# Layer 3 of a four-layer graph network: even bursts of four head units and one outer unit, one accumulator each, and tasks placed by array shape

## The chip, the cores and the metric

The kernel runs on one core of one Trainium2 chip. A core has a matrix engine (PE, with its weight loads shown apart as PEld), a vector engine (DVE), an activation engine (ACT), GpSimd (POOL), and DMA queues, here fed by SyncE (SP). Each engine works through its own instructions in program order and waits for others by semaphores. The metric is the device time of the program in microseconds. Three runs of the kernel before gave 2006.18 to 2008.17 us, median 2007.85.

## The reference

The program is four graph layers over x (16 batches, 1024 nodes, 64 features), with one adjacency matrix; after each layer comes x = layernorm(x + layer(x)). The change touches the fourth, called layer 3:

```
mask = graph + eye(N) > 0
h = einsum('bnc,hdc->bhnd', x, Wh)                 # four heads of 64
out_h = gat(h, mask, bh)                           # per head: softmax over masked h h^T, times h
cat = concatenation of the four heads              # 256
z = leaky_relu(cat, 0.2)
h2 = einsum('bnk,dk->bnd', z, Wo)                  # 64
out2 = gat(h2, mask, bo)                           # the outer attention
z2 = leaky_relu(out2, 0.2)
out = (z2 - mean) * rsqrt(var + 1e-5) * gamma + beta
x = layernorm(x + out)
```

`gat(h)` takes scores h h^T, drops the masked ones, takes a softmax over the neighbours and multiplies by h. Batch b's outer attention needs all four of its heads.

## The kernel before

Names: B = 16 batches, E = 15 the last; P = 128 partitions; N = 1024 nodes, HALF = 512; C = 8 chunks of 128 nodes; D = 64. The four heads are NP = 2 pairs n = 0, 1, the two heads of a pair in the two halves of the 128 partitions.

**Units.** A head unit (`heads`, L1327) is one chunk k of neighbours and one half h of the nodes, for both heads of a pair: two score products into a PSUM tile `s` (L1336; 64 rows by 128 columns of the array each, side by side), an exponential on ACT into `e` (L1340), a multiplication by the adjacency on DVE (`mask`, L1344), and two products with the values into an accumulator y (L1351; 128 rows by 64 columns each). A pair has 16 units: eight chunks for h = 0, then eight for h = 1. Batch b has 32. An outer unit (`head_out`, L1471) is one chunk of the outer attention, with the same four steps and one more on DVE, which adds up the rows (`add_up`, L1489), as the outer attention has no spare column for its sums. Batch b has eight. In the trace each product of 32-bit numbers is two records, so a unit has four records of scores and four of products.

**PSUM.** Pool `ps_s` has three tiles of two banks, tag "s". Scores and every other product of the tasks below take them in turn. Pool `ps_h` has two accumulators, acc0 and acc1. L1349 chooses: pair 0 uses acc0 for h = 0 and acc1 for h = 1, pair 1 uses acc0 for both, and the outer attention acc1. When an accumulator is complete, ACT copies it out (yT, L1358; y2T, L1523).

**Bursts.** The plan (from L1937) cuts the units into bursts, eight for a batch: four of five head units, then four of three head units; in the latter, from batch 1 on, two outer units of the batch before are put between the head units. After batch 15 two bursts with its outer units follow (five and three, LAST = 5). `run` (L1951) emits a burst as: `catch_up` (small steps left over), the scores and exponentials of its units, the tasks of `mids`, the products of the burst before (`drain`), the masks of its own units, and the tasks of `slots`. PE, ACT, DVE and POOL keep this order (`manual_schedule`); the adjacency and sum checks at the end of the program are outside of it.

**Tasks.** Per pair: `project_T` (poT, L1378, shape 64 by 64) turns yT into zT, `inverse` takes the reciprocal of the sums through DRAM, `quotient` multiplies and applies the leaky ReLU. Per batch: `h_2T` (ph2T, L1452, 128 by 64) makes h2 and swaps its halves on DVE; `shift_of` (pn, L1273, 128 by 128) finds the largest norm, whose negative goes into the exponential (DVE, then POOL, then ACT); `h_2v` (ph2v, L1465, 64 by 128) transposes h2 for the values. Then the ends: `gather` (po, L1534, 128 by 128), `layer`, `mean`, `centre`, `scale`, `affine`, `residual`, `mean`, `centre`, `scale`, `finish`, nearly all on DVE, with two small ACT instructions (ln_rstd) after `scale`, which it appends to `roots`; and a Newton step on DVE at the next `catch_up`. Per two batches: `prep_x` (pxT, 128 by 128), `prep_h` (phT, L1310, 64 by 128), `prep_sq`, `prep_v`. Lists of places (from L1850) say in which burst and in which of `mids` and `slots` each task stands. `nodes_adj` (L1253) loads the adjacency for the outer attention in eight pieces, into tiles of the tag "e", and converts it.

The places for the last batches are lists of their own, and the tail after the last burst is an order written out by hand (`ended`, `rest`).

Of the kernel before, what the change touches and what calls it, by code (L numbers as in the profile page):

```python
# [582 lines left out]
def fast_path(  # L583
# [49 lines left out]
    def xb(b):  # L633
        return xg[b // GB][:, :, b % GB, :]
# [61 lines left out]
    def bc_mid(ap, n):  # L696

        return ap.unsqueeze(1).to_broadcast([P, n, ap.shape[1]])
# [98 lines left out]
    def drain():  # L797
        while waiting:
            waiting.pop(0)()
# [451 lines left out]


    def nodes_adj(c):  # L1253
        a_sb = l3.tile([P, N], I32, tag="e", name=f"adj3_{c}", bufs=11)
        nc.sync.dma_start(a_sb, adj_v[c])

        def convert():
            nc.vector.tensor_scalar(
                aN[:, c, :].rearrange("p (k q) -> p k q", q=P), a_sb.rearrange("p (q k) -> p k q", k=C),
                0.0, None, ALU.is_gt,  # L1260
            )
            own = aN[:, c, c * P : (c + 1) * P]
            nc.vector.tensor_tensor(own, own, ident16, ALU.max)

        return convert
    xT2, hTs, shifts, vals, zs, zTs = {}, {}, {}, {}, {}, {}

    def shift_of(key, sq):

        pn = one_bank("pn")  # L1270
        n = sq.shape[1] // P
        for c in range(n):
            nc.tensor.matmul(  # L1273
                pn[:, 2 * c : 2 * c + 2], sq[:, c * P : (c + 1) * P], pair_ones, start=True, stop=True
            )
        top = small.tile([P, 1], F32, tag="top", name="top")
        nc.vector.tensor_reduce(top, pn[:, : 2 * n], AX.X, ALU.max)  # L1277
        gtop = small.tile([P, 1], F32, tag="gtop", name="gtop")
        nc.gpsimd.partition_all_reduce(gtop, top, P, bass_isa.ReduceOp.max)  # L1279
        sh = small.tile([P, 1], F32, tag="shift", name="shift", bufs=6)  # L1280
        shifts[key] = sh

        def below():
            nc.scalar.activation(sh, gtop, AF.Identity, bias=headroom, scale=-1.0)


        soon.append(below)
# [33 lines left out]
    def prep_sq(b, n, h):  # L1321
        cols = slice(h * HALF, (h + 1) * HALF)
        for i in range(2):
            hT, sq = hTs[b + i, n]
            nc.scalar.activation(sq[:, cols], hT[:, cols], AF.Square)

    def heads(b, n):  # L1327
# [18 lines left out]

        def product(k, h, e):
            if k == 0:
                held[h] = ps_h.tile([P, HALF], F32, tag=f"acc{h * (1 - n)}", name=f"y_{b}_{n}_{h}")  # L1349
            for i in range(2):  # L1350
                nc.tensor.matmul(  # L1351
                    held[h][i * D : (i + 1) * D, :], vals[b][:, k, :], e[:, i, :],
# [46 lines left out]
        def project(q):  # L1399

            if q == 0:
                zs[b] = l3.tile([P, C, P], F32, tag="e", name=f"z_{b}", bufs=11)
            pt = ps_s.tile([P, 2, HALF], F32, tag="s", name="po")
            o = pt[:, :, : 2 * (P + 2)].rearrange("p t (c f) -> p t c f", c=2)
            for j in range(CH):
# [24 lines left out]
        return units, [project_T, inverse, quotient]  # L1430


    BURSTS, LAST = 8, 5

    def prep_out(b):

# [6 lines left out]
        def h_2T():  # L1443


            hT = l3.tile([P, 2, HALF], F32, tag="h2T", name=f"h2T_{b}", bufs=1)
            sq = l3.tile([P, HALF], BF16, tag="h2sq", name=f"h2sq_{b}", bufs=1)
            hTs[b] = hT, sq
            pt = one_bank("ph2T")
            for n in range(NP):  # L1450
                for h in range(2):
                    nc.tensor.matmul(  # L1452
                        pt[h * D : (h + 1) * D, :], woT[:, n], zTs[b][:, n, h * HALF : (h + 1) * HALF],
                        start=(n == 0), stop=(n == NP - 1),
                    )
            nc.scalar.copy(hT[:, 0, :], pt)
            nc.scalar.activation(sq, hT[:, 0, :], AF.Square)
            nc.vector.tensor_copy(hT[:D, 1, :], hT[D:, 0, :])
            nc.vector.tensor_copy(hT[D:, 1, :], hT[:D, 0, :])

# [5 lines left out]
            nc.scalar.copy(v, pt)  # L1466
            vals["out", b] = v

        return z_T, h_2T, h_2v

    def head_out(b):  # L1471
        held = {}
# [365 lines left out]

    slots, mids = {}, {}
    work = [[heads(b, n) for n in range(NP)] for b in range(B)]
    outs = [(prep_out(b), head_out(b)) for b in range(B)]
    E = B - 1

    def at(b, j, task, where=slots):
        where.setdefault((b, j), []).append(task)

    for c in range(C):
        convert = {}  # L1850
        at(0, c, lambda c=c, convert=convert: convert.update(go=nodes_adj(c)))
        at((c + 1) // BURSTS, (c + 1) % BURSTS, lambda convert=convert: convert["go"]())
    for b in range(B):
        z_T, h_2T, h_2v = outs[b][0]
        chain = [
            *work[b][0][1], *work[b][1][1], *([z_T] if b == E else []), h_2T,
            lambda b=b: shift_of(b, hTs[b][1]), h_2v,
        ]
        ends = outs[b][1][1]

        places = [(5, mids), (5, mids), (5, slots), (9, mids), (9, mids), (9, slots), (10, mids), (11, mids), (12, mids)]
        places += [(18, mids), *((j, slots) for j in (18, 19, 19, 20, 22, 24, 24, 24, 25, 28))]
        if b == E - 2:
            places[9:] = [(17, mids), *((j, slots) for j in (17, 17, 18, 18, 20, 20, 21, 22, 22, 24))]
        elif b == E - 1:
            places[9:] = [(j, slots) for j in (15, 15, 15, 15, 15, 17, 17, 17, 18, 18)]
        elif b == E:
            places[3] = 7, mids
            places[4:] = [(j, slots) for j in [7] * 5 + [10] * 11]
        for task, (j, where) in zip(chain + ends, places):  # L1870
            t = min(j // BURSTS, E - b)
            at(b + t, j - t * BURSTS, task, where)


    ended = slots[E, BURSTS - 1]
    slots[E, BURSTS - 1] = [ended[i] for i in (5, 0, 1, 6, 2, 3, 7, 8, 9, 4)]
    rest = slots[E, BURSTS + 2]
    slots[E, BURSTS + 2] = [*rest[2:4], rest[0], *rest[4:7], rest[1], *rest[7:]]
    for b in (E - 1, E):
        at(E, 2, lambda b=b: nc.vector.tensor_tensor(xb(b), xb(b), bc_mid(beta, C), ALU.add))  # L1880
    ahead = []
    for b in range(0, B, 2):
        for t, j, task, where in (
            (-1, 3, lambda b=b: prep_x(b), mids),
            (-1, 4, lambda b=b: prep_h(b, 0, 0), mids), (-1, 4, lambda b=b: prep_sq(b, 0, 0), mids),
            (-1, 5, lambda b=b: prep_h(b, 0, 1), mids), (-1, 5, lambda b=b: prep_sq(b, 0, 1), mids),
            (-1, 6, lambda b=b: prep_v(b), slots),
            (-1, 6, lambda b=b: shift_of((b, 0), hTs[b, 0][1]), mids),
            (-1, 7, lambda b=b: shift_of((b + 1, 0), hTs[b + 1, 0][1]), mids),
            (0, 0, lambda b=b: prep_h(b, 1, 0), mids), (0, 0, lambda b=b: prep_sq(b, 1, 0), mids),  # L1890
            (0, 1, lambda b=b: prep_h(b, 1, 1), mids), (0, 1, lambda b=b: prep_sq(b, 1, 1), mids),
            (0, 2, lambda b=b: shift_of((b, 1), hTs[b, 1][1]), mids),
            (0, 4, lambda b=b: shift_of((b + 1, 1), hTs[b + 1, 1][1]), mids),
            (0, 6, lambda b=b: prep_v(b + 1), slots),
        ):
            if b + t < 0:
                ahead.append(task)
            else:
                at(b + t, j, task, where)

    gat = ExitStack()
    gp = gat.enter_context(tc.tile_pool(name="gat2", bufs=2, reuse_waits="tile"))
# [11 lines left out]
        ending = l2_go(extra)  # L1914
    gat.close()
    for j, task in enumerate(ending):
        at(0, j, task)

# [9 lines left out]
    aN = l3.tile([P, C, N], BF16, tag="aN", name="aN", bufs=1)  # L1930
    dram = ctx.enter_context(tc.tile_pool(name="dram", bufs=2, space=bass.MemoryType.DRAM))

    def tasks(where, b, j):
        for task in where.get((b, j), []):
            task()

    plan = []  # L1937
    for b in range(B):
        units = work[b][0][0] + work[b][1][0]
        outer = outs[b - 1][1][0] if b else []  # L1940
        for j in range(BURSTS):
            n = 5 if j < 4 else 3
            burst, units = units[:n], units[n:]
            if j >= 4:
                for i, unit in enumerate(outer[2 * (j - 4) : 2 * (j - 3)]):
                    burst.insert(1 + 2 * i, unit)
            plan.append((b, j, burst))
    units = outs[E][1][0]
    last = [(E, BURSTS, units[:LAST]), (E, BURSTS + 1, units[LAST:])]

    def run(plan):  # L1951
        for b, j, burst in plan:
            catch_up()
            made = [(unit, unit[0]()) for unit in burst]
            tasks(mids, b, j)
            while roots:
                roots.pop(0)()
            drain()
            made = [(product, mask(e)) for (_, mask, product), e in made]
            waiting.extend(lambda product=product, e=e: product(e) for product, e in made)  # L1960
            if (b, j, burst) == plan[-1]:
                drain()
            tasks(slots, b, j)

    with tc.manual_schedule(engines=in_order):
        run(plan)
        run(last)
        for task in [catch_up, *slots[E, BURSTS + 2]]:
            task()


# [73 lines left out]
```

## Time and profile before

The profiled execution took 2005.96 us; its span, from first to last instruction of the core, is 2003.7 us, and the granted PE clock was 0.981 over it.

| stretch (us) | what it is |
|---|---|
| 0 to 650 | layers 0 to 2 |
| 650.0 to 806.95 | layer 3, bursts 0 to 16 |
| 806.95 to 1862.1 | bursts 17 to 120 |
| 1862.1 to 1928.0 | bursts 121 to 126 |
| 1928.0 to 1961.3 | burst 127, and what lies between it and the last outer attention |
| 1961.3 to 2003.7 | last outer attention, and the ends of batches 14 and 15 |

Bursts are counted from 0. A line of PE's timeline gives the start in microseconds, the time that the records take, the line, the tiles written and read with their array shape, and the number of records merged; in brackets stands how long the engine stood idle before, and what ended that. A burst's length is the distance from its first scores to those of the next burst. Some groups of layer 3: masks of heads (L1344) 512 instructions, 599.0 us; exponentials of heads (L1340) 512, 542.6 us; products (L1351) 2048 records, 494.0 us; scores (L1336) 2048 records, 497.3 us.

### The profile page before, as it was taken

The page shows a single profiled execution, that of the slowest core. Times are in us where ns is not written, and L with a number is a line of the kernel's source. Part 1 is how long each engine was busy: PE and PEld are TensorE (multiplying, and loading weights), DVE is VectorE, ACT ScalarE, POOL GpSimd, SP SyncE. Part 2 cuts the span into 40 slices and gives each one's busy share as a digit, 9 for nine tenths or more (in the row PEclk, how much of TensorE's full clock was granted, in tenths as well). Part 3 has the DMA queues.
Part 4 walks back from the last instruction along what each step waited for, and adds up shares of the span by engine and source line. Part 5 has one row for each costly group of instructions (what it writes and reads, how often), then busy time and mean ns, then how long its engine had stood idle before and what let it go on. Part 6 is the DMA issues. An engine that isn't in the chain of part 4 may idle for free.

```text
span 2003.7 us, 25793 instructions
## 1 busy us (share of the span) xinstructions
PE 1891.7 (94%) x9545; PEld 768.3 (38%) x9545; DVE 1764.4 (88%) x2930; ACT 1333.4 (67%) x2343; POOL 81.9 (4%) x77
## 2 busy tenths in 40 slices
PE   7999989998888999999999999999999999999985
PEld 3444447763332333333333333333333333333322
DVE  5899988879999868798898899989989899889996
ACT  5356567767776766676767766766677676776543
POOL 0000000000000000000000000000000000000001
PEclk8999989999999999999999999999999999999997
DMA  7000000000000210000000000000000000100000
GB/s 175 1 1 1 1 1 1 1 1 1 1 1 11 66 31 12 12 22 17 12 17 27 12 17 12 20 26 12 17 12 27 17 12 17 28 12 17 11 17 18
DMA packets 45603, 35.89 MB, mean 18 GB/s; under 512 B 37279, under 2 KB 37344, under 8 KB 45470
## 3 DMA queue, kind: packets, MB, share of 16 engines
q1 hardware_dynamic: 45166, 34.14, 6.6%
q8 instruction: 77, 1.26, 0.3%
q14 instruction: 56, 0.46, 0.1%
q10 hardware_dynamic: 304, 0.03, 0.0%
HBM read 29.45 MB, written 4.70 MB: 17 GB/s over the span
## 4 chain that ended last, share of the span: by engine, by line
PE 61%; DVE 24%; ACT 11%; issue 3%; DMA 1%; POOL 0%; SPq 0%; POOLq 0%; DVEq 0%; ACTq 0%
PE y L1351 16%; PE s L1336 14%; DVE e L1344 8%; DVE e L991 7%; PE y_l L1003 6%; PE po L1776 5%; ACT e L1340 5%; PE y L1504 4%; PE u_l L1015 3%; PE s L1479 3%; ACT e L1484 2%; PE ph2T L1452 1%; PE phT L1310 1%; PE poT L1378 1%; ACT x L780 1%
## 5 line engine op out<-in xcount | busy, mean ns | idle before, releaser
L1340 ACT ACTIVATE e<-s,shift 128x1024 f32<-128x1024 f32 x512 | 542.6, 1119 | 320.1 <-PE s L1336 320.0
L1344 DVE TENSOR_TENSOR e<-e,aT 128x1024 f32<-128x1024 f32 x512 | 599.0, 1215 | 14.8 <-ACT e L1340 14.6
L1351 PE MATMUL y<-e,vals 128*64 128x512 f32 x2048 | 494.0, 605 | 12.5 <-ACT yT L1358 5.9
L1336 PE MATMUL s<-hT 64*128 64x512 f32 x2048 | 497.3, 605 | 1.4 <-ACT e L1340 0.9
L991 DVE SCALAR_TENSOR_TENSOR e<-G_l,q,aT 128x1024 f32<-128x1024 f32 x256 | 315.3, 1275 | 3.9 <-ACT G_l L968 3.9
L1336 PEld LDWEIGHTS s<-hT 64*128 64x128 f32 x2048 | 186.3, 186 | 290.4 <-issue 153.3
L1003 PE MATMUL y_l<-e,vals_l 128*64 128x512 f32 x1024 | 254.2, 616 | 26.9 <-DVE e L991 20.1
L1351 PEld LDWEIGHTS y<-e,vals 128*64 128x64 f32 x2048 | 135.9, 137 | 303.8 <-issue 205.0
L1497 DVE TENSOR_TENSOR e<-e,aT 128x1024 f32<-128x1024 f32 x128 | 156.3, 1225 | 10.4 <-ACT e L1484 1.0
L1489 DVE SCALAR_TENSOR_TENSOR junk<-e,aN 128x1024 bf16<-128x1024 f32 x120 | 146.1, 1217 | 0.0
L1484 ACT ACTIVATE e<-s,shift 128x1024 f32<-128x1024 f32 x128 | 142.0, 1116 | 0.2 <-PE s L1479 0.2
L1504 PE MATMUL y<-e,h2v 128*64 128x512 f32 x512 | 131.6, 597 | 0.6 <-DVE e L1497 0.6
L1479 PE MATMUL s<-h2T 64*128 64x512 f32 x512 | 130.7, 591 | 0.0
L1003 PEld LDWEIGHTS y_l<-e,vals_l 128*64 128x64 f32 x1024 | 62.3, 138 | 160.4 <-issue 75.7
L1776 PE MATMUL po<-hi,aR 128*128 128x512 f32 x256 | 102.7, 402 | 11.2 <-ACT hi L1705 7.3
L1279 POOL PARTITION_ALL_REDUCE gtop<-top x48 | 55.1, 1148 | 1302.0 <-DVE top L1277 996.5
L1776 PE MATMUL po<-lo,aR 128*128 128x512 f32 x256 | 101.1, 396 | 0.0
L780 ACT ACTIVATE x<-m,bn_shift,bn_rstd 128x64 f32<-128x64 f32 x256 | 88.5, 430 | 0.0
L1479 PEld LDWEIGHTS s<-h2T 64*128 64x128 f32 x512 | 49.9, 186 | 60.0 <-issue 26.2
L1383 ACT COPY zT<-poT 64x512 f32<-64x512 f32 x124 | 71.9, 580 | 1.3 <-PE poT L1378 0.2
L1504 PEld LDWEIGHTS y<-e,h2v 128*64 128x64 f32 x512 | 36.5, 137 | 76.0 <-issue 54.0
L978 ACT ACTIVATE vals_l<-x,p 128x64 f32<-128x64 f32 (+1 forms) x256 | 64.3, 339 | 0.0
(252 smaller groups left out, 1874.9 us busy)
## 6 DMA issues: line engine op xcount, KB each, us to landing
r<-inverse SPq DMA_DIRECT2D x62, 256.0 KB
adj<-in_adj_dram SPq DMA_DIRECT2D x16, 512.0 KB
x<-in_x_dram SPq DMA_DIRECT2D x16, 256.0 KB
out_dram<-res SPq DMA_DIRECT2D x16, 256.0 KB
rows<-yT SPq DMA_DIRECT2D x62, 4.0 KB
sums<-rows SPq DMA_DIRECT2D x31, 8.0 KB
inverse<-rt SPq DMA_DIRECT2D x31, 8.0 KB
wl<-in_L_gnn_Wh_dram SPq DMA_DIRECT2D x2, 64.0 KB
```

The costliest lines, as they stand in the source:

```text
L991: nc.vector.scalar_tensor_tensor(e, G[b - b % 2][:, b % 2, :], pq[b - b % 2][1][:, k, b % 2 : b % 2 + 1], aT[:, k, :], ALU.max, ALU.mult,)
L1003: nc.tensor.matmul(held["y"][h * D : (h + 1) * D, :], vals[b][:, k, :], e[:, h * HALF : (h + 1) * HALF], start=(k == 0), stop=(k == C - 1),)
L1336: nc.tensor.matmul(s[:, i, :], hT[rows, k * P : (k + 1) * P], hT[rows, cols], start=True, stop=True)
L1340: nc.scalar.activation(e, s, AF.Exp, bias=shifts[b, n])
L1344: nc.vector.tensor_tensor(e, e, bc_mid(aT[:, k, h * HALF : (h + 1) * HALF], 2), ALU.mult)
L1351: nc.tensor.matmul(held[h][i * D : (i + 1) * D, :], vals[b][:, k, :], e[:, i, :], start=(k == 0), stop=(k == C - 1),)
L1479: nc.tensor.matmul(s[:, i, :], hT[rows, (i + k // CH) % 2, k % CH * P : (k % CH + 1) * P], hT[rows, 0, :], start=True, stop=True,)
L1484: nc.scalar.activation(e, s, AF.Exp, bias=shifts[b])
L1489: nc.vector.scalar_tensor_tensor(junk.rearrange("p c q -> p (c q)").bitcast(BF16), e.rearrange("p i q -> p (i q)"), 1.0, aN[:, k, :], ALU. ...
L1497: nc.vector.tensor_tensor(e, e, aT[:, k, :].rearrange("p (i q) -> p i q", i=2), ALU.mult)
L1504: nc.tensor.matmul(held["o"][h * D : (h + 1) * D, :], vals["out", b][:, k, :], e[:, h, :], start=(k == 0), stop=(k == C - 1),)
L1776: nc.tensor.matmul(po.rearrange("p q k f -> p (q k f)"), aR[:, k, ic * P : (ic + 1) * P], e[:, k].rearrange("p q k f -> p (q k f)"), start ...
```

## The change

The units, their arithmetic and the tasks stay; only their grouping and order in layer 3 change, and some buffers.

- Bursts: twelve of four head units; then 112 of four head units and one outer unit at the end; then five with 4+1, 3+2, 3+2, 3+2 and 3+1 units, outer units between the head units; then the last outer attention (five and three). The outer attention of batch b takes one unit in each of the bursts 8b+12 to 8b+19.
- Accumulators: acc0 for all heads, acc1 for the outer attention.
- Three places in a burst: TOP before the scores, MID between scores and products, END after the products and masks. Within a place an order number sorts the tasks. Tasks with the scores' shape (phT, ph2v) go to END, ahead of the next scores; ph2T goes to the end of MID, ahead of the products; pn, pxT and po go to the start of MID. The `roots` are emptied after MID and END instead of after `mids` alone.
- `h_2T` gives up the swap, which becomes a task of its own one place later; the h2T tile gets two buffers.
- Both shifts of a pair of batches are found in the same MID.
- The adjacency is loaded two pieces at a time, into the buffer of tag "zT", and converted one burst later; z of the last batch takes the tag "xT".
- In the last three bursts the products are not drained ahead of the masks but after them, so that the last outer attention's first five units are finished before the scores of its last three.
- `scale` of batch 13 stands at the END of bursts 127 and 129, its `affine` and first `residual` at the END of 128 and in MID of 129.

```diff
     def nodes_adj(c):
-        a_sb = l3.tile([P, N], I32, tag="e", name=f"adj3_{c}", bufs=11)
-        nc.sync.dma_start(a_sb, adj_v[c])
+        a_sb = l3.tile([P, 2, N], I32, tag="zT", name=f"adj3_{c}", bufs=1)
+        for i in range(2):
+            nc.sync.dma_start(a_sb[:, i, :], adj_v[c + i])
...
-                held[h] = ps_h.tile([P, HALF], F32, tag=f"acc{h * (1 - n)}", name=f"y_{b}_{n}_{h}")
+                held[h] = ps_h.tile([P, HALF], F32, tag="acc0", name=f"y_{b}_{n}_{h}")
...
-            hT = l3.tile([P, 2, HALF], F32, tag="h2T", name=f"h2T_{b}", bufs=1)
+            hT = l3.tile([P, 2, HALF], F32, tag="h2T", name=f"h2T_{b}", bufs=2)
...
+        def swap():
+            hT = hTs[b][0]
             nc.vector.tensor_copy(hT[:D, 1, :], hT[D:, 0, :])
             nc.vector.tensor_copy(hT[D:, 1, :], hT[:D, 0, :])
...
+    TOP, MID, END = range(3)
+
+    def at(burst, place, task, order=5):
+        table.setdefault((burst, place), []).append((order, len(table.get((burst, place), [])), task))
...
+        places = [(5, MID, 3), (5, MID, 4), (7, MID, 4)]
+        if b < E:
+            chain = [*chain, *work[b][1][1], h_2T, swap, lambda b=b: shift_of(b, hTs[b][1]), h_2v]
+            places += [(9, MID, 3), (9, MID, 4), (9, END, 5), (10, MID, 8), (10, END, 5), (11, MID, 0), (12, END, 8)]
+        if b < E - 1:
+            chain = [*chain, *ends]
+            if b < E - 2:
+                places += [
+                    (21, MID, 1), (21, END, 5), (22, MID, 5), (22, END, 5), (23, MID, 5), (24, MID, 5), (24, END, 5),
+                    (25, MID, 5), (26, END, 5), (27, MID, 5), (28, END, 5),
+                ]
+            else:
+                places += [
+                    (21, MID, 1), (21, END, 5), (22, END, 5), (23, MID, 5), (23, END, 5), (24, END, 8), (25, MID, 5),
+                    (25, END, 5), (25, END, 5), (25, END, 5), (26, END, 8),
+                ]
+        for task, (j, place, order) in zip(chain, places):
+            at(g + j, place, task, order)
...
+            (-5, END, 9, lambda b=b: prep_h(b, 0, 0)), (-4, MID, 6, lambda b=b: prep_sq(b, 0, 0)),
+            (-4, END, 9, lambda b=b: prep_h(b, 0, 1)), (-3, MID, 6, lambda b=b: prep_sq(b, 0, 1)),
+            (-3, END, 6, lambda b=b: prep_v(b)),
+            (-2, MID, 0, lambda b=b: shift_of((b, 0), hTs[b, 0][1])),
+            (-2, MID, 0, lambda b=b: shift_of((b + 1, 0), hTs[b + 1, 0][1])),
...
-                n = 5 if j < 4 else 3
...
+    kinds = ["hhhh"] * 12 + ["hhhho"] * (Q * (E - 1) - 4)
+    kinds += ["hhhho"] * 4 + ["hhhho", "hhoho", "hohho", "hhoho", "hohh"]
+    kinds += ["o" * LAST, "o" * (C - LAST)]
...
+    def run(plan):
+        for burst, units in enumerate(plan):
+            catch_up()
+            tasks(burst, TOP)
+            made = [(unit, unit[0]()) for unit in units]
+            tasks(burst, MID)
+            while waiting and burst < len(plan) - 3:
+                waiting.pop(0)()
+            for (_, mask, product), e in made:
+                mask(e)
+                waiting.append(lambda product=product, e=e: product(e))
+            if burst >= len(plan) - 3:
                 drain()
-            tasks(slots, b, j)
+            tasks(burst, END)
```

Here g = 8b, and a place (j, MID, o) stands for burst g + j.

## The prediction

> **What bounds the kernel now.** I read the busy table first, then the busy time by stretch, then PE's timeline burst by burst, and last DVE's and ACT's timelines where PE stood still.
>
> ```profile
> PE 1891.7 (94%) x9545; PEld 768.3 (38%) x9545; DVE 1764.4 (88%) x2930; ACT 1333.4 (67%) x2343; POOL 81.9 (4%) x77
> ...
> 807.00:1862.00 1055.00, 1040.88 (x5038) 377.00 (x5036) 953.88 (x1245) 731.13 (x942) 45.81 (x39) 1.00 0.07 17
> 1862.00:1928.00 66.00, 62.27 (x283) 21.78 (x282) 61.73 (x85) 39.95 (x50) 1.17 (x1) 0.95 0.08 21
> 1928.00:1961.30 33.30, 23.28 (x110) 8.94 (x109) 28.85 (x56) 8.95 (x12) 0.00 (x0) 0.90 0.00 0
> 1961.30:2003.70 42.40, 21.42 (x112) 8.30 (x110) 26.69 (x49) 15.61 (x36) 7.36 (x5) 0.76 0.06 21
> ```
>
> The columns of the stretches are PE, weight loads, DVE, ACT, POOL, clock, DMA. From 807 to 1862 us (bursts 17 to 120) PE is busy 98.7% and DVE 90%: a gain there must shorten PE's own sequence. At both ends of layer 3 PE waits.
>
> ```profile
> 877.55 4.56 PE L1336 MATMUL s<-hT 64*128 64x512 f32 x20
> 882.04 1.08 PE L1351 MATMUL y<-e,vals 128*64 128x512 f32 x4
> ...
> 886.49 4.56 PE L1336 MATMUL s<-hT 64*128 64x512 f32 x20
> 890.98 1.09 PE L1378 MATMUL poT<-yT,wb 64*64 64x512 f32 x8
> 892.00 4.51 PE L1351 MATMUL y<-e,vals 128*64 128x512 f32 x20
> 896.44 4.56 PE L1336 MATMUL s<-hT 64*128 64x512 f32 x20
> ...
> 912.45 0.25 PE L1273 MATMUL pn<-pair_ones,h2sq 128*128 128x2 bf16 x4
> 913.31 1.09 PE L1295 MATMUL pxT<-ident,x 128*128 128x128 f32 x8 [0.61 <-ACT e L1340]
> ```
>
> From first scores to first scores is a burst: 8.94 us without tasks (877.55 to 886.49), 9.95 with poT. Other lengths from this timeline: one pn4 9.12, pn8 9.22, ph2v plus pn8 10.07, ph2T alone 10.66, po plus poT 10.82, phT 9.90. A unit is two times 0.858 us (20 rows of five units, 4.29).
>
> The pxT row shows a rule of the schedule. Five scores and the tasks between share three PSUM tiles, so the first task needs the third exponential, the second the fourth, the third the fifth. ACT takes 5.13 us for five: the second task starts 5.35 us after the burst's start (913.31 less 907.96), the third therefore near 6.36.
>
> ```profile
> 707.42 3.68 PE L1351 MATMUL y<-e,vals 128*64 128x512 f32 x8 [2.61 <-ACT yT L1358]
> 865.89 1.08 PE L1351 MATMUL y<-e,vals 128*64 128x512 f32 x4 [0.41 <-ACT yT L1358]
> 1881.63 1.98 PE L1452 MATMUL ph2T<-zT,woT 128*64 128x512 f32 x4 [3.11 <-DVE zT L786]
> 1883.39 6.60 PE L1351 MATMUL y<-e,vals 128*64 128x512 f32 x20
> 1943.81 1.98 PE L1351 MATMUL y<-e,vals 128*64 128x512 f32 x4 [5.72 <-DVE e L1344]
> ```
>
> These are what the change can take: an accumulator refilled in mid burst while ACT copies it out (707, 865), and DVE late at the end (1881, 1943). After the long ones PE runs at half speed.
>
> **The middle (bursts 17 to 120), part by part.** The built order of PE's instructions gives the tasks of every burst. *One accumulator for heads:* eight units are now two bursts, so the copy of yT falls at a burst's end and has the next scores, 4.3 us, as cover for 0.6 us. That removes 0.57 and 0.28 us per 16 bursts. If ACT were late by 3.7 us the wait would be back. *Tasks by shape:* the stretches of one array shape fall from 375 to 349 in layer 3. The Trainium skill (TensorEngine Tiling (Array Packing), Key Properties) says that a change of tiling mode drains the engine; TensorE: Matmul & The Clock Gate (Single matmul latency) puts the drain near 175 ns, so 26 switches would be 4.6 us, an estimate. The row: pn4 costs 0.18 and pn8 0.28, so four pn are 0.10 and the extra switch 0.08; 26 of them, 2.1 us. I take the row. *Moves within MID:* two shift_of now follow each other (pn16), which costs what ph2v plus pn8 does (10.07 instead of twice 0.28); before ph2T, the third tile, they push it to 6.36: 6.36 + 1.72 + 3.87 + 0.52 = 12.47 us. phT at a burst's end costs 0.86 (no switch) instead of 0.97, ph2v 0.50.
>
> Sixteen bursts then sum as: poT 10.1 (exponentials 0.3 late after phT), 12.47, pn 9.12, ph2v 9.43, po+poT 10.82, three bare 26.8, poT 9.95, pxT+ph2T 12.6, pn+phT 9.98, ph2v+phT 10.3, po+poT 11.0, pn16 10.07, two phT 19.6: **162.2 us**, against 162.6 now (806.95 to 1782.6, six cycles). The 12.6 contains a wait of 1.0: DVE takes 1.135 us per mask of a head (6.89 for six rows) and 2.47 per outer unit, so 7.01 per burst, beside quotient 2.40, centre 1.34, mean 0.92, scale 1.02, layer 1.33, affine 1.34, residual 1.45. From gather, which waits for po at 5.05 us of its burst, to the second quotient four bursts later it needs 49.7 us, while PE's bursts take 47.6: zT comes at 7.2, the second half of ph2T wanted it at 6.3. Six cycles save 2.4 us, the last half cycle 0.8 (78.7 against 79.5): **3.2**. Masks have 2.5 us of slack: they start at most 8 us into a burst and may start 0.8 us into the next.
>
> **The head (650 to 806.95).** Bursts 0 and 1 are bound by ACT; by its rows (four exponentials 4.1, two copies 1.1, squares 1.2 each time) burst 2 begins at 666.2 instead of 668.8. A bare burst of four units is 8.94 - 1.72 = 7.22. Bursts 2 to 16: 8.2 (pn16), 7.2, 7.2, 8.24, three 7.2, 8.24, 9.9, 8.26, 9.43, 9.95, 10.07, 9.8, 9.8 = 127.9. I add 2.2 for the row scaling (2.76 us of ACT) that lands ahead of a burst's exponentials. Burst 17 begins at 796.3: **10.6 less**. But four units, 6.9 us, are still to do; the real gain is 3.7, most of the stall at 707. Adjacency moves from the e ring to one tile of zT, two loads at a time. A load takes 2.1 us (the one issued at 665.45 feeds 666.9 on), two under 5, and the next conversion is a burst of 7.2 away: no cost. If SP held them, 1 to 3 us in each of three bursts, cover gone; I take 0.
>
> **The tail (1862.12 to 2003.7, 141.6 us).** Bursts 121 to 127: 9.95, ph2T 10.66 + 2.0 (no pxT covers zT here), 9.12, 9.43, 10.82, 8.93, 8.93 = 69.8. The 3.1 us wait at 1881 with its half clock goes, since batch 13's ends move to 125 and later.
>
> Burst 128: batch 13's scale stands at the end of 127, and its two ACT instructions (ln_rstd) come ahead of 128's exponentials in ACT's queue. DVE reaches them late: from gather at 5.05 of burst 125: 0.9, masks 8.35, layer 1.33, masks 8.35, mean 0.92, quotient 2.40, centre 1.34, masks 8.35, scale 0.92 = 32.8, PE's three bursts 28.7; 9.2 us into 128. Behind the blocked exponentials waits the fourth score (three tiles), and behind it po and the products of 127: PE idles from 2.6 to 10.95. With half clock until about 16, y of 127 ends at 19.3, and y of 128, waiting for DVE's projection (1.8) and masks, at 22.8. Before, the same place took 23.9 with one unit more (checks, 5.0 us of DVE, 1935.70 to 1940.70). Then 9.4 as now.
>
> The checks now stand between the last five masks and the last three. Behind masks that end at 9.6 us after the first last-outer scores (affine and residual, 2.8, came ahead of them) lie mean, centre, scale 3.3, checks and Newton 5.5, three masks 3.4: 21.7, then product and sums. Now PE is done with sums at 19.3; then at 24.6. PE idles 3.5 us before these products. The clock-gate page (Part 1) says an idle window of about 3.4 us halves the clock; the row at 1881 fell after 3.11. Without the drop +5.3, with it +7; I take 7, by the row. Sum: 69.8 + 22.8 + 9.4 + 42.4 + 7 = 151.4, **9.8 more**, four units of it.
>
> **Sum:** -10.6 - 3.2 + 9.8 = **-4.0 us** on the profiled 2005.96 (span 2003.7 and 2.3 around it). The shown median is 1.9 above that execution; from it, 2003.9.
>
> **Rivals.** *The tail closes up:* if DVE reaches scale with 128's exponentials hardly delayed, burst 128 takes 14 us: -9 more, and 1995. For it: DVE's 0.92 and 1.33 pieces might lie under waits; against: the chain misses by 7 us. Chance 0.24. *The built order does not do it:* excluded, it shows the bursts; a gain of nothing (2007.9) lies in my case. *DVE binds all along (slower):* DVE needs 75.7 us per batch, PE 80.6, with in-order waits for sums (up to 4.3 us into a burst), po and pn in between. It decides once masks start later than 0.8 us into the next burst, my slack of 2.5 used up; then, and at each ph2T, 1.2 us per batch, 14 batches: +17, 2021. For it: 90% busy already, with 26 us of waits for sums; against: the outer units now spread evenly. Chance 0.2, with part of this, 2010 to 2018, the more likely share. My case, 1998 to 2010, has 0.56.
>
> **Numbers.** A measurement here tells 0.2%, 4 us, from no change. My case lies on that edge: of its 0.56, 0.2 is faster, 0.3 within, 0.06 slower. With the rivals: faster 0.44, same 0.31, slower 0.25. The range goes from the tail's rival to half of DVE's.
>
> **What would show it.** Right: no wait of y for yT between 807 and 1850; pn16 bursts of 10.07 and pn16+ph2T of 12.5; a wait of s for ACT e of 8 us near the end, ln_rstd ahead; the last products waiting for DVE behind the checks. Wrong: y waiting for DVE e in the middle, ph2T waiting over 2 us in every batch, or the late wait missing.

## The result, and where the time went

The changed kernel is slower: 2017.94 us as median of four runs (2011.65 to 2019.22) against 2007.01 (2004.02 to 2008.17) for the kernel before; the ratio is 1.0050, 95% interval 1.0026 to 1.0075. On a second chip it was 2012.60 (seven runs) against 2005.45: 1.0049 (1.0031 to 1.0067). The prediction had said 2003.9.

The profiled execution of the changed kernel took 2011.65 us with a span of 2009.4. Layers 0 to 2 are untouched and end within 0.5 us of where they did. The stretches below are cut at the same bursts as before: bursts 0 to 16, 17 to 120, 121 to 127, then burst 128 with what follows it, then the last outer attention with the ends. First the page's busy table and two of its groups, then the busy time by stretch (columns as before: PE, weight loads, DVE, ACT, POOL, clock, DMA).

```profile
PE 1894.7 (94%) x9545; PEld 777.0 (39%) x9545; DVE 1759.5 (88%) x2930; ACT 1336.9 (67%) x2343; POOL 58.8 (3%) x77
...
L1342 PE MATMUL s<-hT 64*128 64x512 f32 x2048 | 477.4, 603 | 10.6 <-ACT e L1346 9.3
L1357 PE MATMUL y<-e,vals 128*64 128x512 f32 x2048 | 473.9, 604 | 0.5 <-ACT yT L1364 0.4
```

```profile
650.00:797.80 147.80, 143.26 (x675) 50.74 (x676) 113.18 (x140) 110.07 (x156) 4.11 (x5) 0.99 0.11 33
797.80:1858.90 1061.10, 1043.97 (x5034) 383.36 (x5030) 948.34 (x1243) 734.13 (x942) 25.46 (x39) 0.99 0.07 17
1858.90:1929.00 70.10, 68.07 (x322) 24.53 (x320) 66.57 (x85) 44.95 (x53) 0.35 (x1) 1.00 0.08 20
1929.00:1961.00 32.00, 21.09 (x102) 8.97 (x101) 23.20 (x41) 7.94 (x11) 0.00 (x0) 0.89 0.00 1
1961.00:2009.40 48.40, 23.87 (x113) 8.48 (x110) 36.72 (x76) 16.13 (x38) 7.16 (x5) 0.77 0.05 18
```

| stretch | before | predicted | measured |
|---|---|---|---|
| bursts 0 to 16 (from 650) | 156.95 | 146.3 | 147.8 |
| bursts 17 to 120 | 1055.15 | 1051.95 | **1061.1** |
| burst 121 to the end | 141.6 | 151.4 | 150.5 |
| sum | 1353.7 | 1349.7 | 1359.4 |

The waits of products for an accumulator's copy are gone from the group of line 1357 (0.4 us), and the long wait of scores for exponentials near the end is there (9.3). Both had been foreseen. The forecast fails in one stretch, the middle: 9.1 us too short. It is also the one stretch where nearly all bursts have the predicted length. The clock of 0.99 instead of 1.00 is a sign of the cause. In the profiled executions the prediction is 9.7 us too low (2001.96 against 2011.65), which the three stretches make up; the medians lie 14.0 apart, and what the profile does not show of that stays open (see below).

The bursts that miss are 34, 50, 66, 82, 98 and 114: 14.37 us each where 12.47 had been worked out. Burst 18 has the same tasks and took 11.78. Here are PE's timelines of both, 18 first.

```profile
807.70 3.70 PE L1342 MATMUL s<-hT 64*128 64x512 f32 x16
811.23 1.02 PE L1488 MATMUL s<-h2T 64*128 64x512 f32 x4
812.19 0.35 PE L1275 MATMUL pn<-pair_ones,hsq 128*128 128x2 bf16 x8
813.05 0.34 PE L1275 MATMUL pn<-pair_ones,hsq 128*128 128x2 bf16 x8 [0.51 <-ACT e L1346]
813.32 1.94 PE L1458 MATMUL ph2T<-zT,woT 128*64 128x512 f32 x8
815.09 3.60 PE L1357 MATMUL y<-e,vals 128*64 128x512 f32 x16
```

```profile
968.99 3.70 PE L1342 MATMUL s<-hT 64*128 64x512 f32 x16
972.52 1.02 PE L1488 MATMUL s<-h2T 64*128 64x512 f32 x4
973.48 0.35 PE L1275 MATMUL pn<-pair_ones,hsq 128*128 128x2 bf16 x8
974.34 0.34 PE L1275 MATMUL pn<-pair_ones,hsq 128*128 128x2 bf16 x8 [0.51 <-ACT e L1346]
975.50 2.64 PE L1458 MATMUL ph2T<-zT,woT 128*64 128x512 f32 x8 [0.82 <-DVE top L1283]
977.91 4.65 PE L1357 MATMUL y<-e,vals 128*64 128x512 f32 x16
```

Two things differ. In burst 34 ph2T waits 0.82 us for DVE's `top`, which frees the PSUM tile of the first pn; DVE reaches `top` only behind quotient. And the same eight records of ph2T take 2.64 us instead of 1.94, the same sixteen of y 4.65 instead of 3.60: 1.75 us more for equal work. DVE's timeline shows the first, the busy time by stretch the second:

```profile
972.88 1.22 DVE L1402 TENSOR_TENSOR zT<-zT,r 128x1024 f32<-128x1024 f32 x1
974.13 1.23 DVE L786 SCALAR_TENSOR_TENSOR zT<-zT 128x1024 f32<-128x1024 f32 x1
975.28 0.25 DVE L1283 TENSOR_REDUCE top<-pn 128x1 f32<-128x16 f32 x2
```

```profile
973.20:976.60 3.40, 2.08 (x24) 1.00 0.00 0
976.60:980.00 3.40, 3.40 (x10) 0.50 0.00 0
980.00:983.40 3.40, 3.40 (x18) 1.00 0.00 0
```

(Columns here: length, PE busy, clock, DMA.) PE had little to do from 973.5 to 975.5, two columns at a time; from 976.6 it ran at half clock for 3.41 us. The same stands in all six bursts, and no half clock stands in the middle of the kernel before.

### The profile page after: what moved, and what is told of

It reads as the page before. It is cut to its first block, busy times and chain, and to the rows that moved or that the text cites. A ratio compares the mean times of both kernels' runs of the same rounds, so it can differ in the third digit from the quotient of the medians.

```text
span 2009.4 us, 25811 instructions
## 1 busy us (share of the span) xinstructions
PE 1894.7 (94%) x9545; PEld 777.0 (39%) x9545; DVE 1759.5 (88%) x2930; ACT 1336.9 (67%) x2343; POOL 58.8 (3%) x77
## 4 chain that ended last, share of the span: by engine, by line
PE 59%; DVE 30%; ACT 6%; issue 3%; DMA 1%; POOL 0%; SPq 0%; DVEq 0%; POOLq 0%; ACTq 0%
PE y L1357 16%; PE s L1342 13%; DVE e L1350 8%; DVE e L991 7%; PE y_l L1003 6%; PE po L1785 5%; PE y L1513 4%; PE u_l L1015 3%; ACT e L1346 3%; PE s L1488 3%; DVE e L1506 3%; DVE junk L1498 2%; PE phT L1316 1%; PE ph2T L1458 1%; ACT x L780 1%
## 5 line engine op out<-in xcount | busy, mean ns | idle before, releaser
L1346 ACT ACTIVATE e<-s,shift 128x1024 f32<-128x1024 f32 x512 | 529.3, 1119 | 164.5 <-PE s L1342 164.5
L1350 DVE TENSOR_TENSOR e<-e,aT 128x1024 f32<-128x1024 f32 x512 | 591.2, 1216 | 12.9 <-ACT e L1346 12.9
L1342 PE MATMUL s<-hT 64*128 64x512 f32 x2048 | 477.4, 603 | 10.6 <-ACT e L1346 9.3
L1357 PE MATMUL y<-e,vals 128*64 128x512 f32 x2048 | 473.9, 604 | 0.5 <-ACT yT L1364 0.4
L1342 PEld LDWEIGHTS s<-hT 64*128 64x128 f32 x2048 | 193.6, 187 | 279.0 <-issue 152.5
L1506 DVE TENSOR_TENSOR e<-e,aT 128x1024 f32<-128x1024 f32 x128 | 156.3, 1225 | 9.5
L1493 ACT ACTIVATE e<-s,shift 128x1024 f32<-128x1024 f32 x128 | 144.4, 1134 | 1.5 <-PE s L1488 1.5
L1364 ACT COPY yT<-y 128x512 f32<-128x512 f32 x64 | 37.5, 586 | 122.4 <-PE y L1357 107.0
L1285 POOL PARTITION_ALL_REDUCE gtop<-top x48 | 32.1, 682 | 1324.3 <-DVE top L1283 953.0
L1325 ACT COPY hT<-phT 128x512 f32<-128x512 f32 x64 | 34.4, 591 | 51.0 <-PE phT L1316 51.0
```

The costliest lines, as they stand in the source:

```text
L1342: nc.tensor.matmul(s[:, i, :], hT[rows, k * P : (k + 1) * P], hT[rows, cols], start=True, stop=True)
L1346: nc.scalar.activation(e, s, AF.Exp, bias=shifts[b, n])
L1350: nc.vector.tensor_tensor(e, e, bc_mid(aT[:, k, h * HALF : (h + 1) * HALF], 2), ALU.mult)
L1357: nc.tensor.matmul(held[h][i * D : (i + 1) * D, :], vals[b][:, k, :], e[:, i, :], start=(k == 0), stop=(k == C - 1),)
L1493: nc.scalar.activation(e, s, AF.Exp, bias=shifts[b])
L1506: nc.vector.tensor_tensor(e, e, aT[:, k, :].rearrange("p (i q) -> p i q", i=2), ALU.mult)
```

## The experiments

Theory T1: pn16 ahead of ph2T makes a pause in PE where DVE is late, the pause brings half clock, and that is the loss of the middle. Rivals: DVE binds the middle anyway, and what is freed comes back as another wait (T2); or the time is lost in the tail alone (T3). The medians of different chips differ by some microseconds, so a ratio is always against the kernel before on the same chip, and parts are compared by the profiled layer 3 (first scores to the end): 1353.7 us before, 1359.0 changed, 1358.8 for the changed kernel on the second chip.

### The changed kernel beside the kernel before again

> The changed kernel as it is, beside the kernel before on the same chip as the next three. If the first comparison holds, 6 to 11 us slower than before (ratio 1.003 to 1.0055), bursts 34, 50, ... again 14.4 with half clock in each.

Ratio 1.0049; bursts 34 and so on 14.38, six half-clock windows. All as in the first profile.

### pn16 behind ph2T

```diff
-            (2, MID, 0, lambda b=b: shift_of((b, 1), hTs[b, 1][1])),
-            (2, MID, 0, lambda b=b: shift_of((b + 1, 1), hTs[b + 1, 1][1])),
+            (2, MID, 9, lambda b=b: shift_of((b, 1), hTs[b, 1][1])),
+            (2, MID, 9, lambda b=b: shift_of((b + 1, 1), hTs[b + 1, 1][1])),
```

> The two norm searches of bursts 18, 34, 50, ... (pn16) stand behind ph2T instead of ahead of it. T1 (ph2T waits there for a PSUM tile that only DVE's top frees, PE is nearly idle for 2.3 us, and half clock follows): bursts 34, 50, 66, 82, 98, 114 fall from 14.37 to about 11.8 us, the six half-clock windows between 950 and 1800 us go, 16 bursts take 161.3 instead of 163.84, and the stretch from burst 17 to burst 121 takes 1046 instead of 1061; the whole is 13 to 16 us faster than the changed kernel, about 2002 to 2004 as median. T2 (DVE limits the middle): ph2T then waits for zT, or y for DVE e, and the burst stays above 13.5; under 5 us are gained. T3 (the loss sits in the tail alone): no gain beyond 3 us.

2002.75 us (12 runs), ratio 0.9992 (0.9981 to 1.0002): the change's loss is gone, by two order numbers in a list of places. No half clock remains in the middle, 16 bursts take 161.9 us, the middle 1048.7 instead of 1061.1, layer 3 1347.2. The burst takes 12.37, not 11.8, since part of T2 is true:

```profile
974.25 1.08 PE L1458 MATMUL ph2T<-zT,woT 128*64 128x512 f32 x4
976.19 1.08 PE L1458 MATMUL ph2T<-zT,woT 128*64 128x512 f32 x4 [0.86 <-DVE zT L786]
977.20 0.55 PE L1275 MATMUL pn<-pair_ones,hsq 128*128 128x2 bf16 x16
```

The second half of ph2T wants zT, which quotient has just finished. PE waits as long as it did for `top`, but half of ph2T has been done by then, and the clock stays up.

### pn16 ahead, in one PSUM tile

```diff
+    def shifts_of(b):
+        pn = one_bank("pn")
+        for i in range(2):
+            shift_of((b + i, 1), hTs[b + i, 1][1], pn=pn[:, 16 * i : 16 * i + 16])
...
-            (2, MID, 0, lambda b=b: shift_of((b, 1), hTs[b, 1][1])),
-            (2, MID, 0, lambda b=b: shift_of((b + 1, 1), hTs[b + 1, 1][1])),
+            (2, MID, 0, lambda b=b: shifts_of(b)),
```

> pn16 stays ahead of ph2T, but both searches write one PSUM tile, so that ph2T takes a tile that an exponential frees and not one that DVE's top frees. T1: the same as with pn16 behind ph2T, bursts 34, 50, ... 11.6 to 11.9 us, no half clock there, 13 to 16 us faster than the changed kernel. Rival (the place ahead of ph2T costs by itself, by the change of shapes or by DVE's top coming late): the burst stays at 13.5 to 14.4 and the half-clock windows stay.

This missed: bursts 34 and so on took 14.57 to 14.65, ratio 1.0047. The edit made the wait that it was to remove. The second pn, which writes another part of the same tile, now waits for the first one's `top`. One of its bursts is worth more than the test: in 114 the wait is as long as in the others, but the clock stayed up, and the burst took 12.95:

```profile
1792.16 0.35 PE L1275 MATMUL pn<-pair_ones,hsq 128*128 128x2 bf16 x8
1794.19 0.34 PE L1275 MATMUL pn<-pair_ones,hsq 128*128 128x2 bf16 x8 [1.68 <-DVE top L1283]
1794.46 1.94 PE L1458 MATMUL ph2T<-zT,woT 128*64 128x512 f32 x8
1796.23 3.60 PE L1357 MATMUL y<-e,vals 128*64 128x512 f32 x16
```

Same order, same wait of 1.68, no half clock: 1.70 us less than the 14.65 of burst 34. So half clock is a separate cost on top of the wait.

### The pause filled with useless products

```diff
+        for _ in range(3 if fill is not None else 0):
+            nc.tensor.matmul(spare, fill[:D, :P], fill[:D, :HALF], start=True, stop=True)
```

> The changed kernel with three useless products of 64 by 512 behind each pn16 that stands ahead of ph2T (their result is read by nobody): about 1.3 us more work for PE in bursts 2, 18, 34, 50, ..., at the place where it waited for DVE's top. If the half clock after the pause is the cost (1.75 of the 1.9 us): no half-clock window between 700 and 1850, bursts 34, 50, ... take 12.9 to 13.1 instead of 14.37 although PE does more in them, burst 18 about 13 instead of 11.8; 16 bursts 162.5. If the wait itself or the place is the cost: 14.4 or more, up to 15.7.

The size was wrong: alone on 64 rows such a product takes 0.92 us (2.77 for three), not the 0.43 that it takes in a pair. So burst 18 and five of the six others took 14.55, burst 82, with the one half-clock window that is left, took 16.20, and the kernel was slower (ratio 1.0097). But burst 18, with no wait to fill, rose by 2.77, and the five by 0.18 only. The next run repeats it with one product.

> As with three useless products, but one alone (0.92 us by that run's rows): it fits into the 0.9 us that ph2T waits for top in bursts 34, 50, ..., so the wait stays as long and only its emptiness goes. If the half clock is the cost: no half-clock windows there, ph2T starts 6.4 to 6.6 us into the burst, as in the changed kernel, and bursts 34, 50, ... take 12.5 to 12.8 instead of 14.37; burst 18 takes 0.9 more (12.7). The middle is 8 to 9 us shorter than in the changed kernel. If the wait itself costs the rest, 14.3 stay.

```profile
978.16 0.35 PE L1275 MATMUL pn<-pair_ones,hsq 128*128 128x2 bf16 x8
979.02 0.34 PE L1275 MATMUL pn<-pair_ones,hsq 128*128 128x2 bf16 x8 [0.51 <-ACT e L1348]
979.29 1.12 PE L1279 MATMUL pn<-hT 64*128 64x512 f32 x2
980.34 1.94 PE L1460 MATMUL ph2T<-zT,woT 128*64 128x512 f32 x8
```

ph2T starts 6.68 us into the burst, 0.17 later than in the changed kernel, and still the burst takes 12.84 instead of 14.37: more work, less time. No half-clock window is left between 700 and 1880. Burst 18 pays 1.06 for the product, the six others gain 1.53 each; 6 x 1.53 - 1.06 = 8.1, and the middle is 8.0 shorter (1053.1). The ratio falls to 1.0011 (1.0000 to 1.0022). This is the direct proof that the half clock, not the wait, is the miss: 1.53 and the 0.17 are 1.70 per burst. Nor is it luck with the clock's grid (last section), on which these bursts stand elsewhere in this run: three windows of 3.41 us (from 815.1, 1139.4 and 1627.5) hold only 1.30 us of other PE work beside the added product, less than the 1.45 after which the changed kernel fell, and full clock follows them.

### That part of the change on the kernel before

```diff
-            (0, 2, lambda b=b: shift_of((b, 1), hTs[b, 1][1]), mids),
-            (0, 4, lambda b=b: shift_of((b + 1, 1), hTs[b + 1, 1][1]), mids),
+            (0, 2, lambda b=b: (shift_of((b, 1), hTs[b, 1][1]), shift_of((b + 1, 1), hTs[b + 1, 1][1])), mids),
...
+                there = mids.setdefault((b, 2), [])
+                there.sort(key=lambda f: f in gathers)
+                there.insert(0, task)
```

> The kernel before with that one part of the change: both norm searches of a pair of batches together, ahead of ph2T in bursts 18, 34, 50, ... (po behind it). There DVE ends quotient 2.2 us into the burst, so top is not late. If the place does harm only where DVE is late: no half-clock windows in these bursts, 11.9 to 12.4 instead of 11.95, and with the 0.3 us saved two bursts later no measurable difference from the kernel before (within 3 us). If pn16 ahead of ph2T does harm by itself: 14 to 14.7 in these bursts, half clock in them, 12 to 16 us slower.

The bursts take 12.52 with no half clock, 0.57 more; 0.63 come back two bursts later (9.44 instead of 10.07). The profiled layer 3 takes 1353.0 instead of 1353.7, but that is partly luck: the middle is 1.7 longer, as bursts 42, 58 and so on take up to 0.7 more, where ph2T now waits for zT; and the head is 2.4 shorter, as the half clock that came with the wait of y for yT at 707 did not come this time. By the ratio, 1.0016 (1.0006 to 1.0026), the kernel is 3.2 us slower, at the edge of the 3 us allowed and far from 12 to 16. In that trace ph2T follows the second pn at once:

```profile
982.06 0.34 PE L1273 MATMUL pn<-pair_ones,hsq 128*128 128x2 bf16 x8 [0.51 <-ACT e L1340]
982.33 1.94 PE L1452 MATMUL ph2T<-zT,woT 128*64 128x512 f32 x8
```

So pn16 ahead of ph2T brought half clock only together with a late DVE. That is new too: in burst 34 of the changed kernel quotient ends 6.4 us into the burst, in the kernel before 2.3.

### The second mean later

```diff
-                    (25, MID, 5), (26, END, 5), (27, MID, 5), (28, END, 5),
+                    (25, END, 6), (26, END, 5), (27, MID, 5), (28, END, 5),
```

> pn16 behind ph2T as before, and the second mean of every batch (0.92 us of DVE) moves from MID of its burst, ahead of the five masks, to the END, behind quotient. If DVE's chain from gather to the second quotient is what makes ph2T's second half wait for zT (0.86 and 0.97), the waits of ph2T shrink to 0 to 0.1 in bursts 34, 42, 50, ... (11.3 and 11.3 to 11.4 instead of 12.37 and 12.29), burst 122 still waits about 0.1; 13 times 0.9: 11 to 12 us off the middle, 1990 to 1992. If DVE is saturated over the cycle, it is late in the next burst and y waits for DVE e, or po's chain moves the wait: under 4 us.

On top of pn16 behind ph2T. Bursts 34, 42 and 122 fall to 11.55, 11.68 and 11.47, the middle to 1040.1, 8.6 less instead of 11 to 12. Bursts 34 and so on gave 0.82 each and bursts 42 and so on 0.61: the latter had waited 0.39 for zT, not the 0.97 expected. In burst 122 a wait of 0.60 is left. 1996.29 us, ratio 0.9963 (0.9948 to 0.9978). So DVE's chain did bind ph2T, but DVE is not saturated: 0.92 us moved behind quotient was time gained, and y waits for no mask in the middle.

### The tail: scale earlier, and the old last order

```diff
-                    (21, MID, 1), (21, END, 5), (22, END, 5), (23, MID, 5), (23, END, 5), (24, END, 8), (25, MID, 5),
+                    (21, MID, 1), (21, END, 5), (22, END, 5), (23, MID, 5), (24, MID, 0), (25, MID, 4), (25, MID, 5),
```

> Only the tail: scale of batch 13 moves from END of burst 127 into MID of burst 128, so that ln_rstd stands behind the exponentials of burst 128 in ACT's queue; its affine moves from END of 128 into MID of 129. If ACT's order is what makes burst 128 long, the 7 us wait of s for ACT e goes, y of 128 ends 16 to 17 us after the burst's first scores instead of 22.1, and the whole gains 4 to 6 us. If DVE's masks set it anyway, the products of 128 wait for DVE e instead and the gain is under 2 us. The middle keeps its six half-clock windows.

Burst 128 takes 27.69 instead of 32.02, y ends 18.2 us after its start instead of 22.7. In the changed kernel this wait stood there:

```profile
1938.77 2.08 PE L1342 MATMUL s<-hT 64*128 64x512 f32 x4 [6.91 <-ACT e L1346]
```

It is gone; two shorter ones of y for DVE e stand in its place (2.22 and 1.33), so DVE was half of it. The last outer attention took 0.8 more, as a half-clock window (from 1957.6) fell on its first scores; layer 3 is 3.3 shorter, not 4 to 6. Against the kernel before the ratio is still 1.0029 (1.0019 to 1.0039). T3 does not hold: the six half-clock windows stayed and the loss with them, while pn16 behind ph2T took the loss away and left the tail as it was.

```diff
-            while waiting and burst < len(plan) - 3:
+            while waiting and burst != len(plan) - 3:
...
-            if burst >= len(plan) - 3:
+            if burst in (len(plan) - 3, len(plan) - 1):
...
-                    (25, END, 5), (25, END, 5), (25, END, 5), (26, END, 8),
+                    (26, END, 3), (26, END, 3), (26, END, 3),
...
+    for i, args in enumerate(early_checks):
+        at(2 + i, END, lambda args=args: check(*args), 7)
```

> Only the tail: the last outer attention gets the order of the kernel before (scores of its last three units ahead of the products of its first five, all eight masks in a row, second norm of batch 13 behind them), and the checks of layers 0 to 2 stand at the ENDs of bursts 2 to 9, where DVE has slack. If the checks between the masks are what costs, the wait of 3.1 us for DVE e at 1980 and the half clock go, and from the last outer scores to the end it takes 42 to 43 instead of 48.4: 5.5 to 6.5 us gained. If DVE's total work sets the end, under 3 us. The ENDs of bursts 2 to 9 cost nothing if DVE has the slack there, else up to 4 us.

From the last outer scores to the end 46.9 us instead of 48.4, a quarter of what was expected, and the ratio is as bad as the changed kernel's (1.0049). PE did gain: its last sums ended 20.7 us after those scores instead of 25.5. But ln_rstd of batch 13 came behind the eight squares of batch 14 on ACT, and the step that waits for it stood ahead of all that was left on DVE:

```profile
1987.49 0.17 DVE L712 SCALAR_TENSOR_TENSOR ln_step<-ln_rstd 128x8 f32<-128x8 f32 x1 [5.09 <-ACT ln_rstd L708]
```

It is the mistake of burst 128 made again, in the edit of the experiment. The checks at the ENDs of bursts 2 to 9 cost nothing: those bursts have the lengths of the changed kernel.

### All mended

The edits above together (without the useless products), and one line more, which puts ln_rstd ahead of the squares:

```diff
+    at(g + 10, END, lambda: roots.pop(0)(), 4)
     for task in (affine, residual, squares):
```

> All at once: pn16 behind ph2T, the second mean later, scale of batch 13 behind the exponentials of burst 128, the last outer attention in the old order with the second root of batch 13 ahead of the squares of batch 14, the checks of layers 0 to 2 in bursts 2 to 9. If the parts are separate: 11 to 12 us below pn16 behind ph2T by the mean, 4 by scale, 5 by the last order, so 1981 to 1985 as median, about 1% faster than the kernel before. If the DVE chain takes back what the middle frees, 1990 to 1995.

1980.59 us (five runs, 1977.37 to 1986.69), ratio **0.9881** (0.9861 to 0.9900): 1.2% faster than the kernel before, and 1.6% than the changed one by the two medians of that chip, just below the 1981 to 1985 us that were expected if the parts are separate. The profiled execution is the longest of the five; its layers 0 to 2, which no edit touches, ended at 656.3 instead of 650. Its stretches are bursts 17 to 120 (cut 0.4 us late: burst 17 begins at 805.13), 121 to 127, 128, and the rest:

```profile
805.50:1845.50 1040.00, 1033.10 (x5032) 379.38 (x5028) 949.03 (x1243) 734.60 (x942) 27.14 (x39) 1.00 0.07 18
1845.50:1914.80 69.30, 68.08 (x322) 24.53 (x320) 66.57 (x85) 45.10 (x53) 0.35 (x1) 1.00 0.08 20
1914.80:1941.40 26.60, 19.23 (x102) 7.92 (x101) 22.69 (x38) 7.95 (x11) 0.00 (x0) 1.00 0.00 1
1941.40:1984.40 43.00, 21.45 (x113) 8.33 (x111) 33.20 (x65) 15.93 (x38) 6.94 (x5) 0.76 0.06 21
```

Against the changed kernel the middle gives 20.7 (1040.4 instead of 1061.1), burst 128 5.4, the last outer attention and ends 5.4. PE is busy 99.3% of the middle (1033.1 of 1040.0), so there only less work for PE would gain more.

## Why the prediction was wrong, step by step

- **One accumulator for heads, right.** Waits of y for yT fell from 5.9 to 0.4 us over the kernel.
- **Bursts without a wait, right.** Bare 8.93, pn4 9.12, po plus poT 10.89 (10.82 predicted), ph2v 9.37 (9.43), pn16 10.07 (10.07). The 0.08 us for a switch of array shape went into such sums; no run measured it alone.
- **zT late for ph2T, right in kind, too large.** 12.29 with pxT (12.6 predicted) and 12.29 in burst 122 (12.66), with waits for zT of 0.39 and 1.41 us (1.0 and 2.0 worked out): zT came 6.9 us into the burst, not 7.2. Moving DVE work ahead of quotient to a place behind it took the first away and left 0.60 of the second.
- **pn16 ahead of ph2T, the step that failed.** The prediction put it as "before ph2T, the third tile, they push it to 6.36: 6.36 + 1.72 + 3.87 + 0.52 = 12.47 us". ph2T started at 6.51, but by another cause: not the fifth exponential holds its tile (in burst 18 it started at 5.62, before that exponential had ended) but `top`, behind quotient. That agreement is chance. The terms that were off are 1.72 and 3.87: at full clock in the sum, at half clock on the chip, 1.75 us more together. So the pause was priced as a wait alone, and the half clock behind it was put at nothing. Six times 1.90 is 11.4; burst 18 gives back 0.7, the other classes 1.6: the 9.1 of the middle. The prediction did weigh half clock, but only at the tail's waits of over 3 us ("the row at 1881 fell after 3.11"). A pause of 0.5 and 0.8 us with pn between was not put under that question. Without the 1.75 the burst would take 12.62, 0.15 over the sum, which is ph2T's later start; the 12.37 with pn16 behind ph2T come from another order with another wait and prove nothing of the sum.
- **The head, right but for 1.5.** 9.2 less instead of 10.6; the row scaling landed ahead of the exponentials of two bursts, 5 and 6, which took 10.07 and 8.14, 2.8 us more than their sums, where 2.2 had been added. The adjacency in pairs cost nothing that shows.
- **The tail, right.** 150.5 against 151.4, with ln_rstd ahead of burst 128's exponentials and the checks between the masks; y of 128 ended at 22.7 (22.8), and the wait of s was 6.9 (8).
- **The rivals.** "The tail closes up" did not happen. "DVE binds all along" named the right engine and the wrong mechanism: masks were never late in the middle; DVE's lateness reached PE through a PSUM tile, and through the clock. In the named price and place (masks over 0.8 us into the next burst, +17) it did not occur. That the median, 2017.94, lies in its milder range of 2010 to 2018 is luck.

**Open:** three of the four timed runs of the changed kernel were 5.6 to 7.6 us longer than the profiled one at about the same mean clock (0.976 to 0.979), and no profile of such a run exists. So of the 14.0 us between the predicted and the measured median the stretches account for 9.7, and the rest is not explained. The kernel with pn16 behind ph2T has a narrower spread (2001.2 to 2005.0 in 12 runs, against 2000.6 to 2011.6 for the kernel before in 38). One long execution was profiled, that of the kernel with all mended: its layers 0 to 2 end at 656.3 us, with 37.6 us of half clock after the first 60 us, where the eleven other traces end at 648.6 to 653.0 with 20.5 to 23.9. Half clock in the earlier layers can thus be a part of the spread; that it was so in the runs of the changed kernel is not shown.

## What to carry to other kernels

A PSUM tile is held until its reader is done, here so late that PE waited 0.82 to 1.68 us: before a product is put behind tiny ones, look at what stands ahead of their reader in its queue, not only at whether a tile will be free. A pause on PE is priced twice, once as a wait and once as the half clock that may follow, and a pause that holds a few small products is still a pause. Work moved on an engine off the critical path can decide it: 0.92 us of DVE per batch behind quotient instead of ahead of it was worth 8.6 us.

## What the runs showed of the hardware

Half clock comes in whole steps of 3.41 us, and all starts of such steps in one trace lie on one grid. So the middle (800 to 1850 us) of nine traces was cut along that grid, and PE's busy time in each window was taken from the matmul records, without those of pn:

| trace | windows with least PE work (us of 3.41) | next window |
|---|---|---|
| changed | six of 1.45 to 1.47; then 2.35 and more | half after the six, full after the rest |
| pn16 in one tile | five of 1.18 to 1.30; one of 1.55; then 2.35 | half after the five; full after 1.55 |
| scale earlier | six of 1.44 to 1.45; then 2.35 | half after the six |
| old last order | one of 1.15, five of 1.45 to 1.46; then 2.35 | half after the six |
| before; pn16 behind; second mean later; one product | none under 2.13 | full |
| three products | none under 2.35 | half after one of 2.57, else full |

All 23 windows with 1.47 us or less (43% of a window) were followed by half clock, none with 1.55 or more, but for one exception with 2.57 us. The three other traces agree: the second of the changed kernel has six windows of 1.45 to 1.46, all followed by half clock, the two others have none under 2.32 and no half clock. The exception lies in the kernel with three products, which use half of the array's rows: its 2.57 us are these products alone. Another window of that trace with 2.79 us, nearly all of them too, was followed by full clock, so what exactly is counted is open. Nor is the border as clean outside the middle: 1.54 us in the kernel before (from 703.3) were followed by half clock, 1.52 us in the kernel with all mended (from 1922.5) were not, and behind the last outer attention of the kernel before even 2.50 us (from 1979.9) were. What surprised is how little it takes: in burst 34 of the changed kernel PE was never idle for more than 0.82 us at a stretch. The Trainium skill (TensorE: Matmul & The Clock Gate, Part 1) gives the window's length, 3413 ns, and that it runs freely; these traces agree. Its table of states asks for an idle window, and a later passage of that part tells, without a figure, of short pauses that were enough in another kernel; here windows that were 43% busy were enough.

The grid also fits burst 114 of the kernel with one tile: there the pause lay across two windows, with 1.55 us of work in the poorer. It fits the wait at 707 too: 2.61 us in the kernel before left the window with 1.54; the same wait (2.62) in the kernel before with pn16 first lay across windows with 2.15 and 2.05, and the clock stayed up. And it tells why all six bursts of the changed kernel fell: they follow each other every 163.88 us, which is 48 steps of 3.413 us (163.84), so the pause stood at nearly the same place of the grid each time.
